# Branches taken from x itself: 1/deviation in one-hot rows, means in the bias rows, rows turned by DMA

## The chip, the cores and the metric

The kernel runs on one core of a Trainium2 chip. The metric is the time of one execution on the device, in microseconds (us); lower is better. Engines are named PE (TensorE matmul), PEld (its weight load), DVE (VectorE), ACT (ScalarE), POOL (GpSimd) and SP (SyncE, which here only issues DMAs).

## The reference, cut to what matters

x has 2 x 2048 tokens of 512 channels. First comes a long front part (a modulated product, a gated recurrence, a gated feed-forward), which the change leaves alone. Its result x2 goes through six branches, of which three are layer norms with gains and biases looked up per token:

```
def _ln(x, g, b): ...  (x - m) * rsqrt(v + EPS) * g + b
h = _ln(x, pw_g[pathway_ids], pw_b[pathway_ids])          # 500 rows
h = _ln(h, cp_g[compartment_ids], cp_b[compartment_ids])  # 5 rows
t = _ln(x, tm_g[time_steps], tm_b[time_steps])            # 5 rows
m, n, r = x + (three vectors, one each per batch row)
s = _ln(x, ms_g[scale_type], ms_b[scale_type])            # 3 rows
w = softmax(aw)
cat = concatenate([w[0]*h, w[1]*t, w[2]*m, w[3]*n, w[4]*r, w[5]*s])   # 6 x 512
out = _ln(silu(cat @ int_W1 + int_b1) @ int_W2 + int_b2, int_g, int_be)
x = x2 + int8_product(out, rhs)
```

m, n and r share x, so the kernel works with four operands: x2 itself, masks (s), times (t) and branch (h). All products but the int8 one are done in f32.

## The kernel before, in words

The front part runs up to about 1392 us and ends with the four calls of `down` (8 tiles of 512 tokens, two per call). Small work for the last part is fitted into `down`'s steps by the table `early`: `load_classes`, `one_hots`, `class_gains`, `class_biases` and others. The last call of `down` also prepares the first tile of the last part (`with tc.high_priority()` at L1625).

The last part is the loop at L1691 over 8 blocks of 512 tokens. Each block has two products, `up` (int_W1) and `down2` (int_W2), and beside them block i+1 is prepared and block i-1 finished:

- `by_tokens` (L1368): 16 PE transposes bring x2 to token-major form (tr_x, copied by ACT L1386 to x2n), DVE takes the statistics (`stats`) and 1/deviation (`rstd_of`, with a square root on ACT). 16 small PE transposes (tr_oh, L1393) turn the one-hot rows of the block's tokens, copied by ACT L1395 to oh. `normed` writes (x-m)*r to ln. POOL gathers gain and bias of the 500-row table from HBM (`gather`, L1361, in order on POOL's own queue); DVE multiplies and adds them (L1408, L1409), takes the statistics again and norms h0 in place with four `normed`.
- `norm_by_channels` and `branch_by_channels` (L1418, L1422) turn ln and h0 back to channel-major form: 16 PE transposes each (tr_l, tr_h), copied by ACT L1346.
- `gains` (L1430): four matmuls of 30 rows multiply the gain table, in three bf16 parts, with the one-hot rows; two DVE multiplications (L1447) apply the result to lnT (n = 0 times, n = 1 masks) and to hT (n = 2).
- `up` (L1453) is a seven-product scheme in place (`paired_in_place`): seven steps of 32 matmuls of 256 columns into banks a, b and d; between steps `tap` reads a bank (on ACT at L1472, or on DVE at L1474 as a difference) before the next step adds to it. DVE forms the sums and differences of operands at L222. `added` (L1482) adds the biases by class: two matmuls per call of 30 one-hot rows against a fourth table, `tables[:, 3]`.
- `down2` (L1513): 16 products of 512 columns for four tiles of 128 tokens, with the next block's `gains` in between.
- `last_norm`, `int8_values` and `int8_product` finish block i-1. `int8_values` turns its bf16 values by a DMA transpose on SP (L1576).

The order on each engine is set when the program is built: a planner goes through the instructions by the order they were traced in and by its own cost model, and moves later work forward where it expects an engine to wait. `tc.issue_after(ins)` pins instructions behind `ins` on its engine; `tc.manual_schedule` keeps PE in the order traced, here for the first block until step 1 of its `up`. SP issues its DMAs in one fixed order. In the first block `up` splits its first two steps in halves, and the table `in_first` says what PE does between these: `times`, `class_sums`, `branch_by_channels`, the branch's gains, `class_bias`. The last two class functions make the bias table from products of the classes' biases with int_W1 (ps_bias and ps_bias_s, L1641 to L1651), and `split` (L1107) cuts it in three bf16 parts on POOL and sends these to `tables`.

Named places of memory (`place`, `carve`) hold the blocks: lnT and tT are shared by all blocks, x2T, x2n and hT alternate between two.

Of the kernel before, what the change touches and what calls it, by code (L numbers as in the profile page):

```python
# [50 lines left out]
def adaln_attn_ffn(ctx: ExitStack, tc: tile.TileContext, a: dict, out: bass.AP):  # L51
# [820 lines left out]
    R = 10  # L872

    onehot = w3.tile([P, NT, G], BF, name="onehot", bufs=1)
    tables = w3.tile([P, 4, D], BF, name="tables", bufs=1)
    idx_pw = w3.tile([P, NT], mybir.dt.int32, name="idx_pw", bufs=1)

    betas_flat = w3.tile([P, 3 * C * R + G - R], FP, name="betas", bufs=1)
    betas = betas_flat[:, : 3 * C * R].rearrange("p (m c r) -> p m c r", c=C, r=R)
# [204 lines left out]
    def one_hots():  # L1084
# [12 lines left out]
        nc.gpsimd.memset(onehot, 0.0)  # L1097
        for k, (lo, hi) in enumerate(((0, 5), (5, 8), (8, 10))):
            shape = [P, NT, hi - lo]
            for n in range(3):  # L1100
                nc.vector.tensor_tensor(
                    onehot[:, :, n * R + lo : n * R + hi],
                    ids[:, k, :].unsqueeze(2).to_broadcast(shape),
                    row_of[:, lo:hi].unsqueeze(1).to_broadcast(shape), ALU.is_equal,
                )

    def split(k, t, parts, engine=nc.vector):  # L1107

        for n, h in enumerate(parts):
            ins = engine.tensor_copy(h, t)  # L1110
            if n < 2:
                engine.tensor_sub(t, t, h)
            for g in range(4 if k < 3 else 1):
                nc.sync.dma_start(tables[G * g + n * R : G * g + n * R + R, k, :], h)
        return ins

    TABLES = (("tm", 0, 5), ("ms", 5, 3), ("cp", 0, 5))

    def load_classes():
        t = held["cls"] = w14("classes")  # L1120
        nc.vector.memset(betas_flat, 0.0)
        nc.vector.memset(t[:R, 0:3, :], 0.0)
        for k, (n, lo, m) in enumerate(TABLES):
            nc.sync.dma_start(t[lo : lo + m, k, :], a[n][:, 0:D])
            nc.sync.dma_start(t[0:m, 3 + k, :], a[n][:, D : 2 * D])

    def class_gains(k):

        t = held["cls"]
        h = t[:R, 6, :].bitcast(BF)  # L1130
        split(k, t[:R, k, :], [h[:, 0:D], h[:, D : 2 * D], h[:, 0:D]])

    def class_biases():

        ps = mm("ps_betas")
        for k, (n, lo, m) in enumerate(TABLES):
            t = held["cls"][:, 3 + k, :]
            for c in range(C):
                p = ps[:, (k * C + c) * 8 : (k * C + c) * 8 + m]
                nc.tensor.transpose(p, t[0:m, ts(c, P)], ident[0:m, 0:m])  # L1140
        for k, (n, lo, m) in enumerate(TABLES):
            nc.vector.tensor_copy(
                betas[:, k, :, lo : lo + m],
                ps.rearrange("p (k c m) -> p k c m", k=16, c=C)[:, k, :, 0:m],
            )

    def steps(*fs):

        def run():
# [11 lines left out]
            4: steps(hidden_columns, (class_gains, 0)),  # L1161
            5: steps(class_biases, (class_gains, 1)),
# [133 lines left out]
    carve(weight("zone_C", "C"), ("x2n0", 8), ("o4_1", 4), ("oh0", 1), ("oh1", 1))  # L1296
# [7 lines left out]
    load_w(w2, a["int_W2"])  # L1304

# [55 lines left out]
    def gather(t, g):  # L1361
        with tc.issue_after(tables_done[0].ins) if J <= t < 2 * J else nullcontext():
            nc.gpsimd.indirect_dma_start(
                out=g, out_offset=None, in_=a["pw"],
                in_offset=bass.IndirectOffsetOnAxis(ap=idx_pw[:, t : t + 1], axis=0),
            )

    def by_tokens(i, k, behind=()):  # L1368
# [20 lines left out]
        with queued(2):  # L1389
            po = tr(f"tr_oh_{i}", BF).rearrange("r a b -> r (a b)")[:, :T]  # L1390
            for j in range(J):
                for g in range(4):
                    nc.tensor.transpose(po[ts(g, G), ts(j, P)], onehot[:, i * J + j], identb)  # L1393
        k["oh"] = place(f"oh{i % 2}", T, dtype=BF)
        nc.scalar.copy(k["oh"], po)  # L1395
        r = rstd_of(mv, f"r1_{i}")
# [3 lines left out]

        ln = k["ln"] = [place(f"o4_{q}", 2, D) for q in PAIRS]
        for q in PAIRS:
            pw = place(f"pw{q}", 2, 2 * D)
            h0.append(pw[:, :, 0:D])
            for j in (0, 1):
                gather(i * J + 2 * q + j, pw[:, j, :])
                normed(ln[q][:, j, :], x2n[:, 2 * q + j, :], mv, r, 2 * q + j)
            nc.vector.tensor_mul(h0[q], ln[q], h0[q])  # L1408
            nc.vector.tensor_add(h0[q], h0[q], pw[:, :, D : 2 * D])  # L1409
            for j in (0, 1):  # L1410
                stats(mv2, 2 * q + j, h0[q][:, j, :], f"s2_{i}")
        r = rstd_of(mv2, f"r2_{i}")
        for j in range(J):
            t = h0[j // 2][:, j % 2, :]
            last = normed(t, t, mv2, r, j)
        return last

    def norm_by_channels(i, k):  # L1418
        for q in PAIRS:
            to_channels(block("lnT"), q, k["ln"][q], f"tr_l_{i}_{q}")  # L1420
# [5 lines left out]
    def by_channels(i, k):  # L1426
        norm_by_channels(i, k)
        branch_by_channels(i, k)

    def gains(i, k, n):  # L1430


        if n == 2:
            dst = src = block("hT", i)
        else:

            src = block("lnT")
            dst = block("tT") if n == (not i) else src
        ps = [tr(f"gain_{i}_{n}_{q}") for q in PAIRS]
        for c in range(C):  # L1440
            of = slice(G * c, G * c + 3 * R)
            nc.tensor.matmul(
                ps[c // 2][:, c % 2, :], tables[of, n, ts(c, P)], k["oh"][of],
                start=True, stop=True,
            )
        for q in PAIRS:
            held["gained"] = nc.vector.tensor_mul(duo(dst, q), ps[q], duo(src, q))  # L1447
# [5 lines left out]
    def up(i, k, then):  # L1453
# [3 lines left out]
        tT, lnT = block("tT"), block("lnT")  # L1457
        masks, times = (lnT, tT) if i else (tT, lnT)
        first, second = (k["x2T"], masks), (times, block("hT", i))
# [22 lines left out]
        def added(n, ps):  # L1482

            o, half = {1: (0, h_a), 2: (0, h_b), 3: (2, h_b), 4: (2, h_a)}[n]
            for u in (0, 1):
                nc.tensor.matmul(
                    ps[u], tables[: 3 * R, 3, ts(o + u, P)], k["oh"][: 3 * R, half],
# [137 lines left out]
    with tc.high_priority():  # L1625
        k = load(0)
        normed_h = by_tokens(0, k, (ends[4], mids[5], ends[6]))
        branch_stats = held["stats"]
# [3 lines left out]
    norm_by_channels(0, k)  # L1632
# [3 lines left out]
    pc = m2_ps.tile([P, D], FP, tag="mm", name="ps_bias_s")  # L1636

    def beta(m, c):
        return betas_flat[:, (m * C + c) * R : (m * C + c) * R + G]

    for m, at in ((0, 0), (2, 2)):  # L1641
        for c in range(C):
            nc.tensor.matmul(
                pb[G * c : G * c + G], beta(m, c), w_int[at + c // 2][:, 1:4:2, c % 2, :],
                start=(m == 0), stop=(m == 2),
            )
    for c in range(C):
        nc.tensor.matmul(
            pc[G * c : G * c + G], beta(1, c), w_int[2 + c // 2][:, 0:3:2, c % 2, :],
            start=True, stop=True,  # L1650
        )  # L1651
    def class_sums():

        pcs = places["k1"]
        nc.scalar.copy(pcs, pc)
        lower, upper = slice(0, 2 * P), slice(2 * P, D)
        with tc.issue_after(normed_h.ins):
            nc.vector.tensor_add(bias, pb, bias)
# [129 lines left out]
```

## Time and profile before

| what | value |
|---|---|
| median of 3 runs | 2020.08 us (2018.74 to 2021.53) |
| profiled execution | 2021.65 us, of which the traced span is 2019.9 us |
| PE busy | 2001.7 us, 99% of the span, 6292 instructions |
| DVE busy | 1174.8 us, 58% |
| ACT busy | 653.4 us, 32% |
| POOL busy | 153.8 us, 8% |
| granted PE clock | 0.996 |
| last part (from 1392.4 us) | 8 blocks, one every 75.9 us in the middle |

The page gives busy times of the whole span; a change that sits in the last part is read in the timelines of that part. Matmuls overlap at their ends, so a busy PE isn't PE at its peak, and what a matmul costs is best taken from one start to the next. Times are counted from the start of the span.

### The profile page before, as it was taken

Reading aid. Unit: us, or ns where it says so; the run is one execution under the profiler, and the core shown is the slowest. Engines: PE = TensorE matmul, PEld = TensorE weight load, DVE = VectorE, ACT = ScalarE, POOL = GpSimd, SP = SyncE. Lnnn points to the kernel's source line nnn. Section 1 sums busy time; section 2 is a strip of 40 time slices with the busy share of each in tenths; the row PEclk is TensorE's granted clock in tenths of the full one; section 3 lists DMA queues with packets and bytes.
Section 4 is the critical chain, followed back from the end, with each engine's and each line's share of the span. In section 5 each row is a group of like instructions: output and inputs, shape, how many; then the busy total and the mean of one; then the engine's idle time right before and its main releaser. Section 6 shows DMA issues by size and latency. Waiting matters only on the chain.

```text
span 2019.9 us, 16905 instructions
## 1 busy us (share of the span) xinstructions
PE 2001.7 (99%) x6292; PEld 1067.4 (53%) x6300; DVE 1174.8 (58%) x1783; ACT 653.4 (32%) x863; POOL 153.8 (8%) x127
## 2 busy tenths in 40 slices
PE   9999999999999999999999999989999999999998
PEld 5444444444444444444444444435877777777774
DVE  6667666666534224324325465466687687687675
ACT  4557777777522222222221000001302302302301
POOL 0141000000400000000010000061300000000000
PEclk9999999999999999999999999999999999999999
DMA  5661212121512112111335766533211211211110
GB/s 202 217 198 52 90 62 98 42 94 58 161 42 91 45 42 94 42 42 52 110 112 180 229 220 224 201 111 130 92 45 63 76 51 63 73 53 63 32 32 21
DMA packets 99332, 197.21 MB, mean 98 GB/s; under 512 B 21393, under 2 KB 49591, under 8 KB 95153
## 3 DMA queue, kind: packets, MB, share of 16 engines
q1 hardware_dynamic: 94584, 179.31, 26.4%
q0 software_dynamic: 4608, 16.78, 2.5%
q8 instruction: 50, 0.82, 0.2%
q14 instruction: 34, 0.27, 0.0%
q10 hardware_dynamic: 56, 0.03, 0.0%
HBM read 133.27 MB, written 58.75 MB: 95 GB/s over the span
## 4 chain that ended last, share of the span: by engine, by line
PE 95%; DVE 1%; issue 1%; POOL 1%; DMA 1%; ACT 0%; SPq 0%; POOLq 0%; ACTq 0%; DVEq 0%
PE up_a L134 16%; PE ps_h_a L134 11%; PE rec_a L134 11%; PE up_d L134 8%; PE dn_a L134 7%; PE ps_h_d L134 6%; PE rec_d L134 5%; PE ps_o L1524 5%; PE up_b L134 4%; PE dn_d L134 3%; PE ps_h_b L134 3%; PE y_a L134 3%; PE rec_b L134 3%; PE dn_b L134 2%; PE y_d L134 1%; PE ps_f L1548 1%
## 5 line engine op out<-in xcount | busy, mean ns | idle before, releaser
L134 PE MATMUL dn_a<-op,w_dn 128*128 128x512 f32 x384 | 169.7, 600 | 5.3 <-DVE op L222 5.3
L134 PE MATMUL up_a<-h,w_up 128*128 128x512 f32 x384 | 172.6, 592 | 0.0
L814 DVE SCALAR_TENSOR_TENSOR prod<-up_d,cols,k 128x512 f32<-128x512 f32 x48 | 36.0, 751 | 199.6 <-ACT k L297 199.6
L297 ACT COPY k<-up_a 128x512 f32<-128x512 f32 x144 | 84.0, 584 | 196.8 <-PE up_a L134 196.7
L794 ACT ACTIVATE gate<-gate,cols 128x512 f32<-128x512 f32 x96 | 68.8, 721 | 215.3 <-DVE gate L793 213.3
L134 PE MATMUL up_a<-h2T,w_up 128*128 128x512 f32 x288 | 129.5, 592 | 0.0
L134 PEld LDWEIGHTS dn_a<-op,w_dn 128*128 128x128 f32 x384 | 72.9, 192 | 95.8 <-issue 87.9
L134 PEld LDWEIGHTS up_a<-h,w_up 128*128 128x128 f32 x384 | 72.9, 190 | 91.9 <-issue 89.7
L134 PE MATMUL rec_a<-h,w_rec 128*128 128x512 f32 x256 | 115.1, 592 | 0.0
L134 PE MATMUL rec_a<-hT,w_rec 128*128 128x512 f32 x256 | 115.1, 592 | 0.0
L1524 PE MATMUL ps_o<-int_w,h 128*128 128x512 f32 x224 | 103.6, 605 | 0.0
L134 PEld LDWEIGHTS up_a<-h2T,w_up 128*128 128x128 f32 x288 | 54.7, 190 | 68.9 <-issue 68.9
L134 PE MATMUL up_b<-h,w_up 128*128 128x512 f32 x192 | 86.3, 592 | 0.0
L134 PE MATMUL up_d<-h,w_up 128*128 128x512 f32 x192 | 86.3, 592 | 0.0
L134 PE MATMUL dn_d<-op,w_dn 128*128 128x512 f32 x192 | 83.7, 594 | 0.0
L134 PEld LDWEIGHTS rec_a<-h,w_rec 128*128 128x128 f32 x256 | 48.6, 190 | 61.2 <-issue 61.2
L134 PEld LDWEIGHTS rec_a<-hT,w_rec 128*128 128x128 f32 x256 | 48.6, 190 | 61.2 <-issue 61.2
L297 ACT COPY k<-rec_a 128x512 f32<-128x512 f32 x96 | 55.7, 580 | 71.1 <-PE rec_a L134 69.5
L793 DVE TENSOR_TENSOR gate<-up_b,k 128x512 f32<-128x512 f32 x48 | 32.9, 690 | 72.2 <-PE up_b L134 71.2
L134 PE MATMUL up_d<-h2T,w_up 128*128 128x512 f32 x144 | 65.2, 592 | 0.0
L1524 PEld LDWEIGHTS ps_o<-int_w,h 128*128 128x128 f32 x224 | 40.2, 189 | 46.5 <-issue 46.5
L222 DVE TENSOR_TENSOR op<-op,op 128x3072 f32<-128x3072 f32 x16 | 55.8, 3486 | 12.3 <-PE dn_d L134 6.5
(403 smaller groups left out, 3444.4 us busy)
## 6 DMA issues: line engine op xcount, KB each, us to landing
pp_d<-prod SPq DMA_DIRECT2D x48, 512.0 KB
op<-pp_d SPq DMA_DIRECT2D x16, 1536.0 KB
y_d<-y SPq DMA_DIRECT2D x16, 512.0 KB
h<-y_d SPq DMA_DIRECT2D x4, 2048.0 KB
yr<-y_d SPq DMA_DIRECT2D x16, 512.0 KB
hs_d<-yr SPq DMA_DIRECT2D x16, 512.0 KB
h<-hs_d SPq DMA_DIRECT2D x4, 2048.0 KB
op<-in_xT SPq DMA_DIRECT2D x32, 256.0 KB
```

Source lines behind the costliest of these rows:

```text
L134: ins = nc.tensor.matmul(ps, ws[k // 2][:, slot, k % 2, ts(u, P)], xs[k], start=(first and k == 0), stop=(last and k == n - 1), skip_group ...
L222: nc.vector.tensor_sub(t, p, q)
L297: nc.scalar.copy(t, ps)
L793: nc.vector.tensor_add(gate[u][:, half], ps, kept)
L794: nc.scalar.activation(gate[u][:, half], gate[u][:, half], AF.Gelu, bias=col("L0_attn_mlp_gate_b", fs[u]),)
L814: nc.vector.scalar_tensor_tensor(prod[u][:, b_], ps, col("L0_attn_mlp_fc_b", fs[u]), kept, ALU.add, ALU.add)
L1524: nc.tensor.matmul(ps, h1[:, c, ts(j, P)], w2[:, c, :], start=(c == 0), stop=(c == C - 1))
L1548: nc.tensor.matmul(ps, qT[:, ts(c, P)], rq[:, c, :], start=(c == 0), stop=(c == C - 1))
```

## The change

For times and masks the norm is now split: (x-m)*r*g + b = x*(r*g) + (-m*r)*g + b. The factor r*g per token and channel comes from one matmul: r, split in three bf16 terms, is put into the one-hot rows in place of the ones, and the tables of gains, also in three bf16 parts, are combined with them in six products (`TERMS`), 30 rows for five classes, 18 for three. x2T is multiplied with it directly, so lnT, `norm_by_channels` and the turned one-hot rows fall away. The branch h does the same with its second norm: h0 is turned without being normed. The terms -m*r per class, 13 classes by 6 products, make 78 more rows of the bias table, so `added` has 108 rows.

The new rows are made by tokens: `as_rows` (seven small DVE operations for each norm), `spread` and `spread_in_groups` (a DVE multiplication with the one-hot values, and an ACT copy into four groups of 32). A DMA transpose on SP, `to_rows`, turns each of the two row tiles z1 (gains of times and masks) and z2 (gains of the branch, and all bias rows): 128 x 1024 bf16 each, as large as what `int8_values` turns.

Around this: `class_gains` writes the six products' rows to HBM and reads them back four times; `class_biases` also transposes the gains; the first block's PE order is gains of masks, ps_bias, half a step, `class_bias`, the branch's transposes, and then times and the branch's gains; the parts of the bias table are cut by ACT and DVE and no longer by POOL, and the gathers of block 1 are no longer pinned behind that; the one-hots are made once instead of three times.

The diff, cut to its core:

```diff
-    R = 10
-    onehot = w3.tile([P, NT, G], BF, name="onehot", bufs=1)
+    R, RB = 10, 23
+    TERMS = ((0, 0), (0, 1), (0, 2), (1, 0), (1, 1), (2, 0))
+    NR = 3 * R + len(TERMS) * (RB - R)
+    onehot = w3.tile([P, NT, R], BF, name="onehot", bufs=1)
...
     def class_gains(k):
-        t = held["cls"]
-        h = t[:R, 6, :].bitcast(BF)
-        split(k, t[:R, k, :], [h[:, 0:D], h[:, D : 2 * D], h[:, 0:D]])
+        m = TABLES[k][2]
+        t = held["cls"][:m]
+        for part in range(3):
+            h = t[:, 6, :].bitcast(BF)[:, ts(part % 2, D)]
+            nc.vector.tensor_copy(h, t[:, k, :])
+            if part < 2:
+                nc.vector.tensor_sub(t[:, k, :], t[:, k, :], h)
+            for q, (_, of) in enumerate(TERMS):
+                if of == part:
+                    nc.sync.dma_start(gains_d[k][q * m : q * m + m], h)
+        rows = len(TERMS) * m
+        for g in range(4):
+            nc.sync.dma_start(tables[G * g : G * g + rows, k, :], gains_d[k])
...
-            4: steps(hidden_columns, (class_gains, 0)),
-            5: steps(class_biases, (class_gains, 1)),
+            4: steps(hidden_columns, class_biases),
+            5: steps((class_gains, 0), (class_gains, 1)),
...
+    for name, n in (("qT0", 2), ("mT", 8), ("pw1", 8), ("q1", 2)):
+        place(name, n * 256)
...
     def gather(t, g):
-        with tc.issue_after(tables_done[0].ins) if J <= t < 2 * J else nullcontext():
-            nc.gpsimd.indirect_dma_start(
+        nc.gpsimd.indirect_dma_start(
...
+    def as_rows(r, mv, name):
+        v = small.tile([P, 2, J], FP, tag="fold", name=f"{name}_v", bufs=2)
+        rows = small.tile([P, 2, J, len(TERMS)], BF, tag="rows", name=f"{name}_rows", bufs=4)
+        nc.vector.tensor_copy(v[:, 0, :], r)
+        nc.vector.scalar_tensor_tensor(v[:, 1, :], mv[:, :, 0], -1.0, r, ALU.mult, ALU.mult)
+        at = 0
+        for n in (3, 2, 1):
+            nc.vector.tensor_copy(
+                rows[:, :, :, at : at + n], v.unsqueeze(3).to_broadcast([P, 2, J, n])
+            )
+            if n > 1:
+                nc.vector.tensor_sub(v, v, rows[:, :, :, at])
+            at += n
+        return rows
+    def by_tiles(name, i):
+        z = place(name, 2, D, dtype=BF).rearrange("p a (j t) -> p a j t", t=P)
+        if not i:
+            nc.gpsimd.memset(z, 0.0)
+        return z
+    def spread(dst, i, of, rows):
+        n = of.stop - of.start
+        oh = onehot[:, i * J : i * J + J, of]
+        return nc.vector.tensor_mul(
+            dst, oh.unsqueeze(2).to_broadcast([P, J, NQ, n]),
+            rows.unsqueeze(3).to_broadcast([P, J, NQ, n]),
+        )
+    def spread_in_groups(dst, i, of, rows):
+        n = of.stop - of.start
+        groups = dst.rearrange("p j (g x) -> p j g x", x=G)[:, :, :, : NQ * n]
+        ins = spread(groups[:, :, 0, :].rearrange("p j (q n) -> p j q n", n=n), i, of, rows)
+        nc.scalar.copy(
+            groups[:, :, 1:4, :], groups[:, :, 0:1, :].to_broadcast([P, J, 3, NQ * n])
+        )
+        return ins
+    def to_rows(dst, src):
+        nc.sync.dma_start(
+            dst.rearrange("p a (j t) -> p (a j) t", t=P),
+            src.rearrange("p a j t -> p (a j t)"), transpose=True,
+        )
...
-        with queued(2):
-            po = tr(f"tr_oh_{i}", BF).rearrange("r a b -> r (a b)")[:, :T]
-            for j in range(J):
-                for g in range(4):
-                    nc.tensor.transpose(po[ts(g, G), ts(j, P)], onehot[:, i * J + j], identb)
-        k["oh"] = place(f"oh{i % 2}", T, dtype=BF)
-        nc.scalar.copy(k["oh"], po)
         r = rstd_of(mv, f"r1_{i}")
+        z1 = by_tiles("q0", i)
+        rows = as_rows(r, mv, f"w1_{i}")
+        spread_in_groups(z1[:, 0], i, slice(0, 5), rows[:, 0])
+        ins = spread_in_groups(z1[:, 1], i, slice(5, 8), rows[:, 0])
+        k["z1T"] = place("z1T", 2, T, dtype=BF)
+        to_rows(k["z1T"], z1)
+        with tc.issue_after(ins.ins):
             for j in range(J):
+                normed(k["ln"][j // 2][:, j % 2, :], x2n[:, j, :], mv, r, j)
...
+        spread(of_means[:, :, :, 0:8], i, slice(0, 8), rows[:, 1])
         r = rstd_of(mv2, f"r2_{i}")
-        for j in range(J):
-            t = h0[j // 2][:, j % 2, :]
-            last = normed(t, t, mv2, r, j)
+        rows = as_rows(r, mv2, f"w2_{i}")
+        spread_in_groups(z2[:, 0], i, slice(0, 5), rows[:, 0])
+        last = spread(of_means[:, :, :, 8:], i, slice(0, 5), rows[:, 1])
+        k["z2T"] = place(f"z2T{i % 2}", 2, T, dtype=BF)
+        to_rows(k["z2T"], z2)
         return last
-    def norm_by_channels(i, k):
-        for q in PAIRS:
-            to_channels(block("lnT"), q, k["ln"][q], f"tr_l_{i}_{q}")
...
-    def gains(i, k, n):
+    def gains(i, k, n, parts=PAIRS):
+        dst = block("hT", i) if n == 2 else block(("tT", "mT")[n])
+        src = dst if n == 2 else k["x2T"]
+        z = k["z2T"][:, 0] if n == 2 else k["z1T"][:, n]
...
-                    ps[u], tables[: 3 * R, 3, ts(o + u, P)], k["oh"][: 3 * R, half],
+                    ps[u], tables[:NR, 3, ts(o + u, P)], k["z2T"][:NR, 1, half],
...
-    norm_by_channels(0, k)
+    gains(0, k, 1)
...
+            h = tab[:RB, part % 2, :]
+            nc.scalar.copy(h, t if part else ps)
+            if part < 2:
+                with tc.issue_after(branch_rows.ins):
+                    nc.vector.tensor_sub(t, t if part else ps, h)
+            nc.sync.dma_start(tables[part * R : part * R + R, 3, :], h[0:R])
+            for q, (_, of) in enumerate(TERMS):
+                if of == part:
+                    at = 3 * R + q * (RB - R)
+                    nc.sync.dma_start(tables[at : at + RB - R, 3, :], h[R:RB])
...
     in_first = {
-        (0, 1, 0): steps(times, class_sums),
-        (0, 1, 1): lambda: branch_by_channels(0, k),
+        (0, 1, 0): steps(class_bias, lambda: branch_by_channels(0, k)),
+        (0, 0, 1): times,
         (1, 0, 0): lambda: gains(0, k, 2),
-        (1, 1, 0): lambda: tables_done.append(class_bias()),
         1: first_block.close,
...
-            then[6] = lambda: by_channels(i + 1, nxt)
+            then[6] = lambda: branch_by_channels(i + 1, nxt)
```

## The prediction

> **What bounds the kernel now.** I read the page first (its first line, the busy shares and the shares of the chain that ended last), then the timelines of PE, DVE, ACT and SP over one steady block, block 3 with block 4 being prepared, then the same over the first block, and the table by windows for the DMA. In the timelines the columns are start, length, engine, line, operation and count, in brackets the idle time before and who ended it; in the last line they are the stretch, its length, busy time and count of PE, PEld, DVE, ACT and POOL, then clock, DMA share and GB/s.
>
> ```profile
> span 2019.9 us, 16905 instructions
> PE 2001.7 (99%) x6292; PEld 1067.4 (53%) x6300; DVE 1174.8 (58%) x1783; ACT 653.4 (32%) x863; POOL 153.8 (8%) x127
> PE 95%; DVE 1%; issue 1%; POOL 1%; DMA 1%; ACT 0%; SPq 0%; POOLq 0%; ACTq 0%; DVEq 0%
> ...
> 1660.29 1.25 PE L1383 MATMUL tr_x<-ident,zone_A 128*128 128x128 f32 x10
> 1661.91 0.41 PE L1393 MATMUL tr_oh<-identb,onehot 128*32 128x128 bf16 x16
> 1662.25 1.56 PE L134 MATMUL ps_h_a<-tT,w_int 128*128 128x256 f32 x6
> 1668.83 0.82 PE L1343 MATMUL tr_l<-ident,zone_A 128*128 128x128 f32 x6
> 1669.72 1.99 PE L134 MATMUL ps_h_a<-x2T,w_int 128*128 128x256 f32 x8
> 1676.83 0.39 PE L1486 MATMUL ps_h_d<-zone_C,tables 30*128 30x256 bf16 x2
> 1677.15 0.44 PE L1343 MATMUL tr_l<-ident,zone_A 128*128 128x128 f32 x2
> 1677.42 0.60 PE L1343 MATMUL tr_l<-ident,zone_C 128*128 128x128 f32 x4
> 1677.86 1.89 PE L134 MATMUL ps_h_a<-tT,w_int 128*128 128x256 f32 x8
> 1684.77 0.60 PE L1343 MATMUL tr_l<-ident,zone_C 128*128 128x128 f32 x4
> 1685.20 1.04 PE L1343 MATMUL tr_h<-ident,zone_B 128*128 128x128 f32 x8
> ...
> 1675.68 0.17 DVE L1327 TENSOR_SCALAR r_rv<-mv 128x4 f32<-128x4 f32 x1
> 1676.93 0.69 DVE L1474 TENSOR_TENSOR zone_B<-ps_h_a,zone_B 128x512 f32<-128x512 f32 x1 [1.09 <-PE ps_h_a L134]
> 1669.08 0.59 ACT L1472 COPY zone_B<-ps_h_a 128x512 f32<-128x512 f32 x1 [4.06 <-PE ps_h_a L134]
> ...
> 1643.01 1.25 SPq L1576 DMA_TRANSPOSE qT<-zone_A  x1
> 1406.00:1408.00 2.00, 2.00 (x14) 1.60 (x13) 2.00 (x3) 0.69 (x2) 0.00 (x0) 1.00 1.10 442
> ```
>
> PE is the path: 95% of the chain. In the steady window 1627.38 to 1703.28 (one block, 75.90 us) it is busy 75.77, DVE 57.36, ACT 16.73. So PE work taken out counts, unless it fills a time in which PE had to wait anyway. Two such times are seen. At **gap B** the next seven-product step accumulates in the bank that ACT L1472 is copying: product matmuls stop at 1668.83 and resume at 1669.72 (0.89), and six tr_l fill exactly that. At **gap C** DVE L1474 must read the bank first: 1676.83 to 1677.86 (1.03), filled by the two class-bias matmuls (0.32) and six tr_l (0.71).
>
> **The change, part by part.** The profiled execution took 2021.65 us (span 2019.9 and 1.75 around it), 1.57 above the median of the three runs, 2020.08. I sum against 2021.65 and take 1.57 off at the end.
>
> *PE work removed in each steady block.* tr_l, 16 transposes, from start to next start: 0.89+0.27+0.44+0.43 = 2.03. tr_oh: 1662.25-1661.91 = 0.34. Together 2.37, seven times (blocks 1 to 7 are prepared inside blocks 0 to 6): -16.6. The gain matmuls keep their 30 or 18 rows and their places; the bias matmuls grow from 30 rows to 108 at the same 256 columns. Here a 30-row bf16 matmul of 256 columns takes 0.16 and a 128-row one of 512 columns (L1548, 8 in 1.73) 0.22, so rows cannot add over 0.06, times 8 a block, and I take nothing.
>
> *Gap B opens.* What could fill it? h0 is not ready (its pair 0 is added up at 1670.0), the x transposes are gone, gains belong to the later step. I charge all 0.89, seven times: +6.2.
>
> *DVE gets longer ahead of gap C.* as_rows is 7 four-element operations per norm; L86, L87, L88 start 0.195 apart, so 1.37. The spreads: nearest row L1101, 0.36 for 160 elements and 0.21 for 64, so z1 0.30+0.23, the means' 0.40, z2 0.30, the last 0.30. Removed: four normed of h0 (L1334, 0.46 apart, 1.84), but those came after gap C. Up to L1327 of the second norm DVE has 1.37+0.53+0.40 = 2.3 more, and had 1.08 of idle time. It would reach L1474 at 1677.98 to 1678.15 while PE is ready 0.34 earlier than before (no tr_oh), at 1676.49. PE resumes 0.93 after L1474's start, near 1679.08: a gap of 2.59. To fill it: 0.32 of bias matmuls and the 16 tr_h (1.95 as 8 in 0.97). They can go there since h0 is no longer normed, so ready by 1675.4 (1673.5 plus 1.9 for as_rows and the z1 spreads) and not at 1680.8. That leaves 0.3 if the planner puts all 16 there, nothing if it slips L1474 between two statistics: 0.15, seven times, +1.0.
>
> *ACT.* Off: two copies of 1.01 and one of 0.60. On: four bf16 copies of 120 to 360 elements, between 0.2 and L1395's 0.6 each. Net nothing or a gain; z1's copies end by 1668.5, just ahead of L1472. If one collides, up to 0.46 a block; in the range.
>
> *SP, POOL and the turned rows.* Two DMA transposes more per block. The row: qT's two issues (1.24 each) start at 1643.01 and 1644.54 and the DMA engines are busy from 1644 to 1647, so 2.6 from issue to data for eight 128x128 squares. z1 (1668.5) is turned by 1671 and needed at 1686; z2 (ready 1683.3) by 1686 and needed by gains(2) near 1694.7. Queued behind on SP is only the x2T load, which waits on PE until 1675.2 in any case; POOL's gathers start some 7 us earlier, as tr_h does, and collide with nothing due. The Trainium skill speaks against this step: VectorE: DVE Perf Modes, "Rules for kernel authors", would transpose 128x128 on TensorE where PSUM can take it, and "The three transpose paths" gives the DMA 1309 ns per 128x128 bf16 square. Eight squares would be 10.5: z2T at 1695, 0.3 late per block (+2), and 7.9 late in the first block; the total would be about no change. The measured 2.6 decides.
>
> *Before the loop.* class_biases has 24 transposes for 12: those 12 took 0.83 (L1140, 1142.91 to 1143.74), +0.75. class_gains sends 30 DMAs for 36, a third of them over DRAM: SP waits for those to land, with loads of op behind it; 0 to 3 us, I take 0, since PE ran without a pause in that stage.
>
> *The first block,* 1392.40 to 1417.36, where PE waited 1.15. Less work: tr_oh 0.34, tr_l 1.89, bias products 24 in 2.72 now 16 in about 1.6. PE alone would end near 1411.9. But gains(2) needs z2T. DVE starts its branch when the gathers land (1391.56) and was full until 1409; second statistics, now with mask products and the bias sum slipped in between, end near 1403.4, the second rstd 1404.2, rows and spreads 1406.2, ACT copy 1406.7, issue and data 2.6: 1409.3 with a free queue. (pw1 also moves to another place, on buffers of the stage before that may still be being stored at 1386; its gathers could land 2 us later, and pair 1 is first touched at 1396.55, so nothing. The two POOL memsets of z, 0.95 for 1024 elements at L1097, run while POOL has nothing else.) It is not free: the loads of rows, int_W2 and x2T, issued 1399.6 to 1401.9 on SP's queue, keep the engines busy to 1410 (share 1.10 in the line shown), so z2T lands at 1411.6 at the earliest. Moreover block 1's gathers no longer wait for the tables: they start near 1402, on another queue. The skill (DMA: Bandwidth & Descriptors, "Queues, rings and completion order") says each engine takes its queue rows in turn; then 5 us of the gathers' 7.5 come in front and z2T lands at 1416.5. By the queue's own row alone 1411.6; I take 1413. From there 5.6 us of PE remain (0.33 gain matmuls, 1.73 behind the tensor_mul, 3.5 of hT): 1418.6, so +1.2, between -0.2 and +4.7.
>
> Sum: -16.6+6.2+1.0+0.75+1.2 = -7.45, so 2014.2, and on the median's scale **2012.6**.
>
> **Rivals.** 0.2% (4 us) is about what a measurement of this kernel can tell from no change.
>
> *D, slower: the planner leaves tr_h behind the last step.* Where the removed tr_l were traced (after step 6), tr_h is traced too, and before ran at 1685. DVE's longer chain then holds gap C open for 2.27 with nothing in it: -2.37+0.89+2.27 = +0.79 a block, +5.5, with +1.95 from the rest +7.5: 2027.6. It decides from the point where fewer than nine of the sixteen move up ((10.4-1.95)/7 = 1.2 unfilled). Against it: the planner pulled six tr_l from the same place into each gap.
>
> *C, no change: half moves, or the first block runs into the gathers.* Eight tr_h leave 1.3 open, -0.2 a block: +0.6 in all, 2020.7; or +4.7 in the first block: 2016 with full gains elsewhere.
>
> *B, the whole removal counts.* Gap B finds filler or the tap comes sooner and the first block gains: -16.6+0.75 = -15.9, 2004.2.
>
> *DVE as the new bound*: 57.4-1.84+2.74+1.53 = 59.8 of 74.5 us. Not seen as a case.
>
> **How the numbers follow.** The sum as worked out (2009 to 2016) 0.50; B 0.12; C 0.20; D 0.18. Faster by over 0.2%: the sum and B, 0.62. Within: C and a little of D, 0.21. Slower: 0.17. The range runs from B to the far side of C, 2004 to 2022, and leaves D out.
>
> **What would show it.** Right: no tr_l or tr_oh; block period between 74.4 and 74.8; PE idle near 0.9 at the copy of the second tap in each block; tr_h between steps 5 and 6; the two new DMA transposes of a block landing within 3 us of issue. Wrong: tr_h after step 6 with PE waiting for L1474's successor; PE waiting for the gain matmuls of the second branch in steady blocks; a wait of over 6 us in the first block.

## The result, and the profile after

| | before | after |
|---|---|---|
| median of 14 runs each | 2019.28 us (2016.52 to 2021.53) | 2019.15 us (2016.11 to 2023.43) |
| ratio after to before, 95% interval | | 1.0001 (0.9994 to 1.0009) |
| profiled execution, its span | 2021.65, 2019.9 | 2017.25, 2015.4 |
| one block in the middle | 75.90 | 74.12 |
| granted PE clock, whole span | 0.996 | 0.993 |

The change made no difference to the time. The two profiled executions differ by 4.4 us, more than the medians do. So totals are taken here from medians and ratios, and traces only for what happens inside a stage.

The page of the kernel after: the span, the busy times, and the shares of the chain that ended last.

```profile
span 2015.4 us, 16584 instructions
...
PE 1978.2 (98%) x6056; PEld 1053.9 (52%) x6064; DVE 1181.0 (59%) x1899; ACT 647.2 (32%) x872; POOL 147.7 (7%) x123
...
PE 91%; DVE 6%; DMA 1%; ACT 1%; issue 1%; POOL 0%; SPq 0%; DVEq 0%; POOLq 0%; ACTq 0%
```

PE has 23.5 us less work than before (2001.7), but the span is only 4.5 shorter: PE now waits where it didn't wait before. The chain passes through DVE for 6%, where it was 1%.

*The steady block.* PE's timeline of the kernel after, the same place in the block that was shown of before (columns: start, length, engine, line, operation, count, in brackets the idle time before and who ended it).

```profile
1644.44 0.38 PE L1557 MATMUL ps_h_b<-z2T,tables 108*128 108x256 bf16 x2
1644.66 1.89 PE L134 MATMUL ps_h_d<-tT,w_int 128*128 128x256 f32 x8
...
1672.04 1.99 PE L134 MATMUL ps_h_a<-x2T,w_int 128*128 128x256 f32 x8 [0.73 <-ACT zone_B L1543]
...
1679.05 0.82 PE L1358 MATMUL tr_h<-ident,zone_B 128*128 128x128 f32 x6
1680.38 0.38 PE L1557 MATMUL ps_h_d<-z2T,tables 108*128 108x256 bf16 x2 [0.51 <-DVE h L1566]
1680.59 0.38 PE L1358 MATMUL tr_h<-ident,zone_B 128*128 128x128 f32 x2
1680.81 0.38 PE L1358 MATMUL tr_h<-ident,pw 128*128 128x128 f32 x2
...
1688.06 0.82 PE L1358 MATMUL tr_h<-ident,pw 128*128 128x128 f32 x6
```

No tr_l and no tr_oh are left. The first line comes once a block, here 74.12 after the last (1570.32). Gap B, where ACT must copy a bank before PE adds to it, is open by 0.73 at 1672.04. Gap C, where DVE must read one, holds 10 of the 16 tr_h and the two bias matmuls, with 0.51 of waiting; the last six tr_h stay behind step 6. The wait stands ahead of the bias matmuls, and it ends with a DVE instruction ahead of the third tap (L1545): L1566 reads bank d, to which the bias matmuls add.

```profile
1679.66 0.66 DVE L1566 TENSOR_TENSOR h<-ps_h_d,zone_B 128x512 f32<-128x512 f32 x1
```

The view of PE's waits has both gaps in seven of the eight blocks:

```profile
PE gain L1516 <- DMA z2T<-q: 8.2, 1, 8.2
...
PE ps_h_a L134 <- ACT zone_B L1543: 5.1, 7, 0.7
...
PE ps_h_d L1557 <- DVE h L1566: 3.7, 7, 0.6
```

The columns are us in total, times, longest. The first line is the surprise: one wait in the first block, nearly as long as all fourteen at the two gaps together (8.8).

*The first block.* PE's timeline of the kernel after:

```profile
1392.41 3.22 PE L1718 MATMUL ps_bias<-w_int,betas 128*32 128x512 f32 x32
...
1408.19 1.13 PE L134 MATMUL ps_h_b<-tT,w_int 128*128 128x256 f32 x4 [1.69 <-DVE tT L1520]
1409.16 1.03 PE L134 MATMUL ps_h_d<-tT,w_int 128*128 128x256 f32 x4
...
1419.22 0.61 PE L1516 MATMUL gain<-z2T,tables 30*128 30x512 bf16 x4 [8.17 <-DMA z2T<-q]
1419.77 3.32 PE L134 MATMUL ps_h_b<-tT,w_int 128*128 128x256 f32 x8
...
1426.38 1.03 PE L134 MATMUL ps_h_d<-tT,w_int 128*128 128x256 f32 x4
```

SP's timeline there, and the first of POOL's four gathers of block 1 (the last was issued at 1404.96):

```profile
1399.48 1.28 SPq L1312 DMA_DIRECT2D rows<-in_rows  x3
1400.87 0.38 SPq L59 DMA_DIRECT2D int_w<-in_int_W  x1
1401.34 0.45 SPq L1373 DMA_DIRECT2D x2T<-x  x1
...
1406.81 5.01 SPq L1425 DMA_TRANSPOSE z2T<-q  x1
```

```profile
1401.11 1.06 POOL L1377 DMA_INDIRECT zone_B<-in_pw,idx_pw  x1 [7.39 <-PE tr_h L1358]
```

And the table by windows (stretch, its length, busy time and count of PE, PEld, DVE, ACT, POOL, then clock, DMA share, GB/s):

```profile
1408.00:1410.00 2.00, 1.81 (x8) 1.52 (x9) 1.87 (x3) 0.19 (x1) 0.00 (x0) 1.00 1.03 428
...
1412.00:1414.00 2.00, 0.00 (x0) 0.00 (x0) 0.00 (x0) 0.02 (x1) 0.00 (x0) 1.00 1.55 291
1414.00:1416.00 2.00, 0.00 (x0) 0.00 (x0) 0.00 (x0) 0.60 (x1) 0.00 (x0) 0.91 0.55 122
1416.00:1418.00 2.00, 0.00 (x0) 0.00 (x0) 0.00 (x0) 0.00 (x0) 0.00 (x0) 0.50 1.24 292
...
1420.00:1422.00 2.00, 2.00 (x5) 1.61 (x6) 2.00 (x2) 0.00 (x0) 0.00 (x0) 0.50 0.00 0
```

z2T's transpose was issued at 1406.81 and PE could use it at 1419.22, 12.4 us later; PE waited 8.17 of them. The DMA engines were full until 1412; then they moved less, with a lull of 122 GB/s from 1414 to 1416, and were not done until after 1418. Before, they were nearly idle from 1410 on. After the wait PE's clock was 0.50, and the eight products at 1419.77 took 3.15 to the next start (1422.92), where before eight of them took 1.82 (1408.77 to 1410.59).

The length of the stage: before, from tr_oh (1392.40) to step 2 of `up` (1417.36), 24.96. After, from the first gain matmuls (1392.09) to the rest of step 2 (1426.38), 34.29; the first four of that step's 32 products, 0.86, had been done in between (1409.16), so 33.43 is to be compared. The stage grew by 8.5. From there on the profile after is faster: block 0's remainder by 1.4, each steady block by 1.78.

### The profile page after: what moved, and what is told of

It is laid out like the page before. It is cut to its first block, busy times and chain, and to the rows that moved or that the text cites. A ratio compares the mean times of both kernels' runs of the same rounds, so it can differ in the third digit from the quotient of the medians.

```text
span 2015.4 us, 16584 instructions
## 1 busy us (share of the span) xinstructions
PE 1978.2 (98%) x6056; PEld 1053.9 (52%) x6064; DVE 1181.0 (59%) x1899; ACT 647.2 (32%) x872; POOL 147.7 (7%) x123
## 4 chain that ended last, share of the span: by engine, by line
PE 91%; DVE 6%; DMA 1%; ACT 1%; issue 1%; POOL 0%; SPq 0%; DVEq 0%; POOLq 0%; ACTq 0%
PE up_a L134 16%; PE rec_a L134 11%; PE dn_a L134 8%; PE up_d L134 8%; PE ps_h_a L134 6%; PE ps_h_d L134 6%; PE rec_d L134 5%; PE ps_o L1595 5%; PE up_b L134 4%; PE dn_d L134 3%; PE y_a L134 3%; PE ps_h_b L134 3%; PE rec_b L134 3%; PE dn_b L134 2%; DVE s_st L1335 2%; PE y_d L134 1%
```

## The experiments

**Theory.** The steady gain is real and was given back in the first block: z2T's transpose stands in the DMA engines with SP's own 2.75 MB of loads (rows, int_W2, x2T of block 1) ahead of it and block 1's 2 MB of gathers beside it. **Rivals:** the order of SP's queue alone; the gathers alone; a transpose of such small rows is slow in itself; DVE's chain is late, not the DMA.

### Gathers out of the way

```diff
+        with tc.issue_after(held["mark"].ins) if J <= t < 2 * J else nullcontext():
             nc.gpsimd.indirect_dma_start(...)
...
+        if not i:
+            held["mark"] = nc.gpsimd.tensor_copy(seen, k["z2T"][:, 0, 0:8])
```

> The changed kernel with one thing undone in the first block: block 1's four gathers wait on POOL until z2T has landed, so they share no DMA engine with its transpose. The changed kernel itself takes 2019.2 us; there PE waits 8.2 us for z2T (landed near 1419), and its clock falls to 0.50 after it. Theory (loads ahead on SP's queue and gathers beside it share the delay): z2T lands at 1411.6 to 1412.5, the wait is 1 to 2 us, the clock stays at 1.0; 7 to 8.5 us less, 2011 to 2012. Rival (SP's own queue alone): landing and time unchanged, 2019. Rival (the gathers alone): the landing goes to 1410 or earlier, no wait, 2009.5. Rival (a transpose of small rows is slow in itself, about 12 us from issue): landing not before 1417, 2017 to 2019. Rival (DVE is late, not the DMA): tT's wait stays and the gain is under 2 us.

Measured: 2011.6, ratio to before 0.9963 (0.9950 to 0.9976). SP's row of the issue, and PE's timeline:

```profile
1406.43 2.14 SPq L1426 DMA_TRANSPOSE z2T<-q  x1
```

```profile
1412.98 0.40 PE L1520 MATMUL gain<-z2T,tables 30*128 30x512 bf16 x4 [2.31 <-DMA z2T<-q]
```

6.55 us from issue to use instead of 12.4, a wait of 2.31, and the eight products behind in 1.83 (1413.30 to 1415.13). The landing is 0.5 later than the range that was expected. The result rules out SP's queue alone (no change expected) and the gathers alone (no wait expected).

### Loads out of the way

```diff
-    for k in range(3):
-        nc.sync.dma_start(rows[:, k, :], ...)
-    load_w(w2, a["int_W2"])
...
+    with tc.issue_after(held["turned"].ins):
+        first_next = load(1)
+        for n in range(3):
+            nc.sync.dma_start(rows[:, n, :], ...)
+        load_w(w2, a["int_W2"])
```

Here `held["turned"]` is z2T's transpose.

> The changed kernel, with SP's loads of x2T of block 1, rows and int_W2 (2.75 MB) issued behind z2T's transpose and not ahead of it; block 1's gathers stay where they are, beside it. Theory (both share the delay): the transpose is issued early and meets only the gathers; it lands at 1409.5 to 1412, 7 to 9 us less, 2010 to 2012. Rival (SP's queue alone): the same or a little better, landing near 1409.4. Rival (the gathers alone): the landing moves by less than 2 us, 2017 to 2019. Rival (slow in itself): landing not before 1417, 2017 to 2019. The bias tables' four DMAs now stand behind the loads on SP's queue and may be late for the bias matmuls by up to 2 us.

Measured: 2008.38, ratio 0.9947 (0.9934 to 0.9960). Issue at 1407.36:

```profile
1412.66 0.40 PE L1513 MATMUL gain<-z2T,tables 30*128 30x512 bf16 x4 [1.07 <-DMA z2T<-q]
```

5.3 us from issue to use. The landing is 0.7 later than expected and the time 1.6 below the expected range. Again most of the loss is gone, by taking away the other of the two transfers.

### Both out of the way

The two edits above in one kernel.

> Both: block 1's gathers behind z2T's landing on POOL, SP's loads of x2T of block 1, rows and int_W2 behind its issue. Nothing is in the DMA engines beside the transpose. Theory: z2T lands at 1409.4 to 1410, PE doesn't wait for it, block 0's step 2 starts 9 us earlier than in the changed kernel: 9.8 us less, near 2009.4. If the transpose is slow in itself: a wait of 6 us or more stays, 2015 to 2019. What may spoil it: the bias tables behind 2.75 MB of loads, needed near 1417; if they land at 1418 to 1420, 2011 to 2012.

Measured: 2012.48, ratio 0.9968 (0.9955 to 0.9981), no better than either alone. SP's row of the issue, and POOL's of the small copy that reads z2T, which shows the landing:

```profile
1406.21 1.26 SPq L1423 DMA_TRANSPOSE z2T<-q  x1
```

```profile
1409.02 0.19 POOL L1495 COPY seen<-z2T 128x8 bf16<-128x8 bf16 x1 [15.92 <-DMA z2T<-q]
```

PE's timeline and the table by windows show where the time went:

```profile
1424.95 0.59 PE L1558 MATMUL ps_h_b<-z2T,tables 108*128 108x256 bf16 x2 [2.74 <-DMA int_w<-in_int_W]
```

```profile
1424.00:1426.00 2.00, 1.05 (x6) 0.90 (x7) 0.36 (x1) 0.00 (x1) 0.00 (x0) 0.65 0.03 13
```

With empty engines the transpose lands 2.81 us after its issue and PE doesn't wait for it: it is not slow in itself. But the last parts of the bias table now stand on SP behind int_W2 (issued 1409.97), and the bias matmuls, which read tables and not int_w, wait 2.74; the row names the load that stands ahead of these parts in the queue. After that wait the clock is 0.65, and from the bias matmuls to the second group of step 3's products PE takes 4.31 where the next kernel takes 3.11. The expectation named the late tables and allowed them 2 us or so; it left out the clock.

### Loads behind the bias table too

```diff
+        with tc.issue_after(held["last_table"].ins):
+            load(1)
+            for n in range(3):
+                nc.sync.dma_start(rows[:, n, :], ...)
+            load_w(w2, a["int_W2"])
```

This and the last three kernels below have the two edits above as well, with this order of the loads.

> As the one with both, but SP's loads of x2T of block 1, rows and int_W2 stand also behind the bias tables' four DMAs, so that neither z2T nor the tables are behind them. Theory: no wait of PE in the first block for z2T or for the tables, 2009 to 2010, and level with or up to 2 us better than the one with both. If int_W2, now last, is late for its first use in block 0 (after 1457 in the changed kernel), PE would wait there; 2.75 MB took about 8 us, so it should land before 1425 and cost nothing. Rival (slow in itself): 2015 to 2019.

Measured: 2007.78, ratio 0.9944 (0.9930 to 0.9958), 1.2 below the expected range. The transpose was issued at 1407.97; POOL's row of the landing, and PE's of the two users of z2T:

```profile
1410.77 0.19 POOL L1495 COPY seen<-z2T 128x8 bf16<-128x8 bf16 x1 [15.72 <-DMA z2T<-q]
```

```profile
1412.14 0.40 PE L1517 MATMUL gain<-z2T,tables 30*128 30x512 bf16 x4
...
1423.80 0.39 PE L1558 MATMUL ps_h_b<-z2T,tables 108*128 108x256 bf16 x2
```

No wait of PE for z2T, for the tables or for int_W2. The runs in one table; the last column runs from the start of ps_bias to the rest of step 2 (1426.38 in the kernel after):

| beside or ahead of the transpose | issue to use or landing | ps_bias to step 2 |
|---|---|---|
| loads ahead and gathers beside (the change) | 12.4 | 33.97 |
| loads ahead | 6.55 | 26.98 |
| gathers beside | 5.3 | 25.82 |
| nothing, table late | 2.81 | 24.88, then 2.74 of waiting |
| nothing | 2.80 | 24.68 |

DVE's chain is not it either: the wait for tT, 1.7 in the kernel after, is 1.6 to 1.7 in all of these, while the time falls by 7 to 11 us. Alone the loads add 3.7 and the gathers 2.5; together they add 9.6, which is 3.4 more than the sum. The Trainium skill (DMA: Bandwidth & Descriptors, "Queues, rings and completion order") says that an engine takes the queue rows in turn and starts what stands in one row in its order. A delay from each of the two fits that; the 3.4 does not follow from it. One thing beside it can be seen: the lull in the kernel after (122 GB/s from 1414 to 1416, against 428 from 1408 to 1410), while z2T and part of the gathers were still to come. The two kernels below that leave both transfers in place have it in the same stretch, at 104 (PE kept busy) and 44 GB/s (30 rows). What makes it, and how much of the 3.4 it is, is not shown by these runs.

### PE kept busy during the wait

```diff
+    def kept_busy():
+        ps = m2_ps.tile([P, D], FP, tag="mm", name="ps_idle")
+        for n in range(18):
+            nc.tensor.matmul(ps, ident, k["x2T"][:, n % C, :], start=True, stop=True)
...
-        (1, 0, 0): lambda: gains(0, k, 2),
+        (1, 0, 0): steps(kept_busy, lambda: gains(0, k, 2)),
```

> The changed kernel with 18 matmuls more in the first block, identity times x2T into a bank that nobody reads, put into PE's order right before the branch's four gain matmuls, that is into the wait for z2T. It tells apart what the wait itself costs and what the clock's fall to 0.50 after it costs. Theory: z2T lands as before, 12 us after its issue, the idle time before the gains shrinks to near 0 with the 18 in it, and the eight matmuls behind take 1.73 and not 3.15, the clock staying at 1.0: step 2 of block 0 starts 1.5 us earlier after ps_bias's start than in the changed kernel (33.97). Rival: the low clock has another cause than PE's idling (then it falls there all the same, and nothing changes).

Measured: 2023.13 in one run. PE's timeline:

```profile
1410.14 15.61 PE L1752 MATMUL ps_idle<-zone_A,ident 128*128 128x512 f32 x36
1425.69 0.39 PE L1516 MATMUL gain<-z2T,tables 30*128 30x512 bf16 x4
1426.02 1.99 PE L134 MATMUL ps_h_b<-tT,w_int 128*128 128x256 f32 x8
...
1431.30 1.89 PE L134 MATMUL ps_h_d<-tT,w_int 128*128 128x256 f32 x8
```

The filler was mis-sized: an f32 matmul of 512 columns runs as two passes of 0.43, so 18 of them took 15.6 us and not 8, and outlasted z2T. The total is therefore no answer, but the part behind it is: from the gains to the next start of step 2 PE took 5.61 at clock 1.00, as with the short wait of 2.31 (1412.98 to 1418.59 with the gathers late), and 7.16 after the wait of 8.17. The low clock comes from PE's idling and cost 1.55 us. The profile of before has such a fall too, 35 us ahead of the first block: a wait of 5.32, with the clock at 0.50 from 1356 to 1360.

```profile
1357.33 12.79 PE L134 MATMUL dn_a<-op,w_dn 128*128 128x512 f32 x24 [5.32 <-DVE op L222]
```

### The bias matmuls with 30 rows

```diff
-  ps[u], tables[:NR, 3, ts(o + u, P)], k["z2T"][:NR, 1, half],
+  ps[u], tables[: 3 * R, 3, ts(o + u, P)], k["z2T"][: 3 * R, 1, half],
```

> The changed kernel with the 78 rows of the means left out of the bias matmuls, so that these have 30 rows as they had before the change: the biases' mean part is left out of the result. Theory: the rows themselves cost PE something apart from columns: a pair with 108 rows starts 0.22 before what follows, a pair with 30 rows took 0.31 before the change, and the products behind it 0.1 more. Then the block's period grows from 74.12 to 74.7 to 74.9. Rival (a matmul's price is its columns alone, the 0.19 per pair lies in the places of the pairs): the period stays within 0.1 of 74.12. The prediction's own bound (more rows cost up to 0.06 each): the period falls by up to 0.5.

Measured: 2022.18 in one run; a block every 74.55 instead of 74.12. PE's timeline of this kernel:

```profile
1647.10 0.39 PE L1557 MATMUL ps_h_b<-z2T,tables 30*128 30x256 bf16 x2
1647.42 1.99 PE L134 MATMUL ps_h_d<-tT,w_int 128*128 128x256 f32 x8
1649.25 1.89 PE L134 MATMUL ps_h_d<-hT,w_int 128*128 128x256 f32 x8
```

With 30 rows the pair takes 0.32 and the group behind it 1.83; with 108 rows (1644.44 above) 0.22 and 1.73. So the change's more rows made these matmuls cheaper, by 0.43 a block: the theory's sign, but less than its 0.6 to 0.8. That one of the four pairs sits in gap C, where PE waits for DVE anyway, may be part of the reason; it was not tested.

### The place of pw1

```diff
-    for name, n in (("qT0", 2), ("mT", 8), ("pw1", 8), ("q1", 2)):
+    for name, n in (("qT0", 2), ("pw1", 8), ("mT", 8), ("q1", 2)):
```

> As the one with the loads behind the bias tables (2007.8), and pw1 placed ahead of mT in memory, so that block 0's gathers of pairs 2 and 3 don't wait for the store of dk (5.4 to 5.8 us of POOL's waiting, DVE's second pair then 2.3 us later than before the change). Theory: DVE's chain was the next thing late: PE's waits for the second pair's transposes (0.8) and for tT (1.6) go, z2T's rows come 2 us earlier, and 2 to 2.4 us fall away: 2005.4 to 2006. Rival (mT, which now lies on that buffer, is late in its place, or DVE is full there in any case): same as 2007.8 within 1.

Measured: 2007.25, ratio 0.9938 (0.9925 to 0.9952). POOL's wait of 5.8 for the store of dk is gone, and so is PE's wait of 0.8 for the second pair's transposes; ps_bias to step 2 is 23.83, 0.85 less. The time as a whole is level with the one before (0.9944), as the rival had it. The wait for tT stayed as it was:

```profile
1406.33 1.13 PE L134 MATMUL ps_h_b<-tT,w_int 128*128 128x256 f32 x4 [1.58 <-DVE tT L1521]
```

So little more than a third of the expected gain came, and in the stage only: DVE has hardly a gap there in any case.

### Gap B filled

```diff
-            then[3, 0] = lambda: int8_product(i - 1, qs[0], last["x2n"], 1, held["ins"])
+            then[4] = lambda: int8_product(i - 1, qs[0], last["x2n"], 1, held["ins"])
```

In this kernel the sum with x2n for these tokens comes after x2n's place has been overwritten by the tokens of the block being prepared, so that part of the output is another; the instructions and their sizes are the same.

> As the one before it in this call, and in blocks 1 to 7 the second half of the int8 product (eight matmuls, 1.73) stands behind step 4 of up and not within step 3, so that PE has it to do while ACT copies the second tap (gap B, open by 0.73 since the change). Theory: gap B closes six times, 4.4 us; gap C may close as well since DVE's part of that product no longer stands ahead of the second statistics, up to 0.5 six times: 4.4 to 7.4 us less than the one before it, near 1999. Rival (DVE's two multiplications and the sum, 2.2 us, now stand between the second norm's work and the third tap): gap C opens by as much as gap B closes, no change.

Measured: 2007.38, ratio 0.9939 (0.9925 to 0.9953), level with the one before; the period is 73.91 for 74.13. DVE's timeline around the third tap, then PE's:

```profile
1666.31 0.72 DVE L1623 SCALAR_TENSOR_TENSOR zone_C<-ps_f,qs,rsbc 128x512 f32<-128x512 f32 x1
...
1667.02 0.74 DVE L1623 SCALAR_TENSOR_TENSOR zone_C<-ps_f,qs,rsbc 128x512 f32<-128x512 f32 x1
...
1668.41 1.22 DVE L1660 TENSOR_TENSOR zone_C<-zone_C 128x1024 f32<-128x1024 f32 x1
...
1669.63 0.68 DVE L1546 TENSOR_TENSOR zone_B<-ps_h_a,zone_B 128x512 f32<-128x512 f32 x1
```

```profile
1668.47 0.38 PE L1558 MATMUL ps_h_d<-z2T,tables 108*128 108x256 bf16 x2 [0.91 <-DVE h L1567]
...
1670.37 1.99 PE L134 MATMUL ps_h_a<-tT,w_int 128*128 128x256 f32 x8 [0.43 <-DVE zone_B L1546]
```

Gap B closed and gap C opened: the waits there went from 0.51 to 0.91 and 0.43. The rival was right: 2.7 us of DVE's work on the product now stand ahead of the third tap, L1546.

### Gap B filled, DVE's sums behind the tap

```diff
+            then[2] = steps(
+                lambda: int8_product(i - 1, qs[0], last["x2n"], 0, held["ins"]),
+                lambda: keep_x(i - 1, last["x2n"]),
+            )
+            then[4] = lambda: held.update(pss=int8_matmuls(i - 1, held["ins"]))
+            then[6, 0] = lambda: int8_sums(i - 1, qs[0], held["pss"])
```

`keep_x` is POOL's copy of the pair of x2n; `int8_matmuls` and `int8_sums` are the two halves of `int8_product`.

> As the one with the eight matmuls of the int8 product in gap B (2007.4), with DVE's part of that product moved behind the third tap, into step 6: POOL keeps the pair of x2n that the sum needs by a copy, in the place of the values already rounded. It tells whether the 2.7 us that DVE spent on that product ahead of the third tap is what opened gap C by as much as gap B closed. Theory: gap B stays closed, DVE reaches the third tap 1.7 us earlier than in the kernel with pw1's place changed (2007.25, block's period 74.13), so gap C's wait of 0.51 goes as well: period 72.9 to 73.4, six blocks, 4.5 to 7.5 us less, 2000 to 2003. Rival (DVE's sums, now behind the tap, delay the rows of the branch's norm or the first gains, or the banks held longer stop PE at down2): period 74 or more, 2007 or more.

Measured: 2002.05, ratio 0.9910 (0.9897 to 0.9924): 0.9% faster than before, and the best of all kernels here. The period is 73.03. PE's timeline at gap C:

```profile
1664.96 1.89 PE L134 MATMUL ps_h_a<-mT,w_int 128*128 128x256 f32 x8
1667.29 0.38 PE L1558 MATMUL ps_h_d<-z2T,tables 108*128 108x256 bf16 x2 [0.45 <-DVE h L1567]
1667.51 0.82 PE L1355 MATMUL tr_h<-ident,zone_B 128*128 128x128 f32 x6
1668.17 1.89 PE L134 MATMUL ps_h_a<-tT,w_int 128*128 128x256 f32 x8
```

Gap B stays closed in six of the seven blocks. Gap C kept a wait of 0.45, where the theory expected none, but it is shorter: from the end of step 5's products (1666.69, the last start plus 1.73) to step 6 PE takes 1.48 with six tr_h in it; in the kernel with pw1's place changed it took 2.00 with ten, so most of that difference is the four tr_h that now stand elsewhere. DVE did not reach the tap sooner in its own chain: from the first statistics of the block to the third tap it takes 15.71 in both kernels, and 18.4 with the sums ahead of the tap. Of the 1.10 won per block 0.73 is gap B; how the rest divides was not taken further.

## Why the prediction was right or wrong

The measured time lies in the range, but the likeliest case, 7.5 us faster, did not come. What came is the second form of rival C, the first block that runs into the gathers, with both of its terms larger than written: more won in the blocks, more lost in the first. That the sum of the two lies in the range is partly luck: the blocks won some 3 us more than worked out (0.45 in each of seven), the first block lost 7.3 more.

- **The steady block: right mechanism, a little too small.** Predicted -1.33, measured -1.78. Gap B opened by 0.73 (taken as 0.89). Gap C has 0.51 (taken as 0.15): of the sixteen tr_h ten went there and not all. What ends that wait was not seen: the bias matmuls were counted as filling (0.32), but they wait for DVE L1566 themselves. What was left out is what they cost. The step "rows cannot add over 0.06, times 8 a block, and I take nothing" bounded the cost from above only; 108 rows take less than 30, and the run with 30 rows puts 0.43 a block on that; with it the sum comes to -1.56 (-2.37 + 0.73 + 0.51 - 0.43), and 0.2 stays open. The step's own two numbers spoke against it: 0.16 for 256 columns with 30 rows, and 0.22 for 512 columns, twice as many, with 128 rows.
- **Rival D fell.** The planner moved more than nine tr_h up, the point that the rival named.
- **z2T's rows: right.** The ACT copy was to end at 1406.7; SP issued the transpose at 1406.81. The 2.6 us from issue to data also held wherever the engines were free (2.8). The price of one square in the Trainium skill (VectorE: DVE Perf Modes, "The three transpose paths"), which the prediction multiplied to 10.5 for eight, does not add up so for eight sent as one.
- **The landing in the first block: the step that failed.** "By the queue's own row alone 1411.6; I take 1413": it was 1419.2. The two loads were known and both bounds were worked out (1411.6 and 1416.5), but the value was taken near the lower one although the gathers' start near 1402 was a part of the change and in plain sight; and the upper one was too low as well, since the two delays do more than add. The term +1.2 measured +8.5, 7.3 more: 6.2 from the later landing, 1.55 from the next point and 0.3 since the stage began that much earlier, less the 0.86 of step 2 that was done during the wait. One of the signs of being wrong, a wait of over 6 us in the first block, had come.
- **The clock: not in the sum.** After the wait PE ran at 0.50, worth 1.55. The profile of before shows the like behind its wait of 5.32, and the Trainium skill (TensorE: Matmul & The Clock Gate, "Why this matters for your kernels") warns of PE idling over about 3 us between bursts. This belonged beside the upper bound: a landing at 1416.5 would have meant some 5 us of idle PE. The runs agree for 8.17 (0.50) and 2.31 (1.00); with 2.74 the clock already fell (0.65, then 0.50), earlier than that rule of thumb says.
- **ps_bias:** "24 in 2.72 now 16 in about 1.6" compared the trace's count of before with the code's count of after. The trace counts two passes for each f32 matmul; after has 32 in 3.15, 1.6 more than taken. As PE waits for z2T in any case, it cost nothing until that wait was gone. Two sums beside it are off: with its own terms PE alone would end near 1412.9 and not 1411.9, and the twelve transposes of class_biases, 0.83 in the trace, went in as 0.75.
- **pw1's gathers:** "so nothing" was wrong in the mechanism. They waited 5.4 for the store of dk, and DVE's second pair came at 1398.87 and not at 1396.55; hidden behind z2T here, and worth 0.85 in the stage when it no longer is.

With nothing in z2T's way (2007.78) the change is worth 0.56% (0.9944), 11 us, more than the 7.5 predicted, and most of it is what the first block ate: 9.3 from ps_bias to step 2. The profiled pair alone would have said 4.4 us faster; the fourteen runs of each, which spread over 5 and 7 us, say no difference. Where this spread lies was not found: the length of the wait for z2T is one place that varies (8.17 here, 9.19 in the run with 30 rows, whose first block has the same order).

## What to carry to other kernels

A transfer that comes onto the critical path must be priced with everything that is queued ahead of it and beside it at that moment, its own data being the smallest part: 2.8 us of transpose became 12.4. When a pin is taken away (here that of block 1's gathers), ask which transfers now start earlier and whom they meet; putting the bulk transfers behind the small urgent one won back 11 us with the same work. And a filler for a gap brings its work on other engines with it: the same eight matmuls were worth nothing with DVE's sums ahead of the next tap, and 5 us with the sums behind it.

## What the runs showed of the hardware that I had not expected

- The transpose's issue on SP took 5.01 us with loads ahead and gathers beside, 2.14 with the loads alone ahead and 1.24 to 1.28 otherwise, and what stands behind it on SP (parts of the bias table) is issued later by as much.
- Two bf16 matmuls of 256 columns with 108 rows between f32 products of 128 rows cost up to 0.2 us less than with 30 rows, half of it in the products that follow.
- A wait of PE of 2.74 us was followed by a granted clock of 0.65 (1424 to 1426) and 0.50 (1426 to 1428), one of 2.31 by none below 1.00.
- With the loads ahead of the transpose and the gathers beside it, the DMA engines fell from some 400 GB/s to 122, 104 and 44 in the same 2 us of three traces, with work still to come.
